# Block 0's sums on GpSimd cut to one and one copy given to ScalarE, next rows requested ahead of the kept transpose, last offset sums held: one change in three parts

## Chip, cores, metric

The kernel runs on one core of a Trainium2 chip. The metric is the device time of one execution in microseconds (us), median over several executions.

## The reference

Two layers of a small graph network over 128 graphs of 64 nodes with 768 features, all in float32:

```python
h = relu(layernorm(x))
for l in range(2):                                   # 2 layers
    m_left, m_right = h @ W_left[l].T, h @ W_right[l].T
    u = lower/upper mix of (h @ m_left.T) and (h @ m_right.T), / sqrt(768)
    attention = exp(u) * adj, each row divided by its sum
    ctx = attention @ (h @ W_lin[l].T + b_lin[l])
    h = relu(ln_a[l] * (ctx - mean) / (std + 1e-3) + ln_b[l])
return x + h
```

(The lines are shortened; shapes are x 128 x 64 x 768, adj 128 x 64 x 64, each weight 2 x 768 x 768.)

## The kernel before

The rows are cut into 16 blocks of 512. A product of 768 x 768 is split into 3 x 3 x 2 pieces and done with 15 instead of 18 groups of multiplications, so each block needs sums of weight pieces (once a layer) and sums of token pieces (once a block). TensorE does the groups, GpSimd most token sums, VectorE and ScalarE the rest. Three places matter here.

The first block. Rows arrive in four tiles; each gets statistics (VectorE), a shift column `nb` (VectorE), a scaling (ScalarE), six transposes (TensorE) and copies out of PSUM. Then the weight and token sums must be ready before TensorE's groups:

```python
START = (0, 2, 1, 3)
# in transpose_rows(0, 0): statistics, column and scaling of tile after tile, then
def turn(n, q):                 # transposes of tile q, then two copies out
    ...
    for m, p in enumerate(banks):
        ...
        (nc.vector.tensor_copy if n < 2 else nc.scalar.copy)(to, ...)
for n, q in enumerate(START):
    todo.append(lambda n=n, q=q: turn(n, q))
...
# the sums; GpSimd's are held until a column is done, by a small copy that reads it
ws, vs = sums_w(0, "l", nc.gpsimd), sums_w(0, "l", nc.vector)
hold(KEEP["nb"][:, START[-2]:START[-2] + 1])
for f in ws[:2]:                # two weight sums on GpSimd
    f()
t, w = deque(sums_t((1, 0, 0), nc.vector)), deque(vs[2:])   # all others on VectorE
needs = ("twtwt", "ttwww", ...)  # what VectorE does ahead of which group
```

The block change. During block u, the rows of block u+1 are normalised, transposed and stored ("kept") in DRAM; the kept transpose is read back as `ht`, and the rows of block u+2 are requested into the freed row tiles. All of these requests stand in one queue, SyncE's:

```python
todo = transpose_rows(l, u, sp)            # ends with the four stores
todo.append(lambda: load_h(1, l, u))       # ht: reads the kept transpose back, 1536 KB
if u + 1 < NB:
    todo.append(lambda: load_rows(l, u + 1, sp))   # eight tiles of 192 KB
...
todo.append(lambda: load_adj(u))           # two transfers of 128 KB
```

The last block. The residual rows and the offset are added ahead of time on GpSimd, at two slots of the plan:

```python
for xs, slot in zip(XS[u, 1], (26, 45)):
    put(slot, lambda xs=xs: nc.gpsimd.tensor_add(xs, xs, rows["b"]))
```

## Time and profile before

| | before |
|---|---|
| time, median of 3 (later 4) executions | 2754.47 us, 2753.4 to 2755.24 (2754.31) |
| span of the profiled execution (a separate one; it took 2756.64 us, more than any of those) | 2754.9 us |
| TensorE busy | 2730.8 us, 99% |
| TensorE idle, all of it | 24.1 us |

How to read it: in the profile's lines PE is TensorE, PEld its weight loads, DVE VectorE, ACT ScalarE, POOL GpSimd and SPq SyncE's queue of requests; L429 is line 429 of the kernel's file, and X, Y, Z, V and aux name banks of PSUM. The bracket behind a TensorE row gives the idle time before it and what ended it. Two more readings of the kernel before: first the transfers of the rows, from the last part of the page (KB each, median us from issue to landing):

```profile
x<-in_x_dram SPq DMA_DIRECT2D x120, 192.0 KB, 8.3
```

Then the stretch around the first scores, in windows of two microseconds: the window and its length, the busy time of PE, PEld, DVE, ACT and POOL with their instructions, the granted TensorE clock, the DMA engines' busy share (a transfer is counted where it starts, so it can pass 1), GB/s.

```profile
70.00:72.00 2.00, 2.00 (x83) 1.67 (x85) 1.93 (x6) 0.00 (x0) 1.92 (x2) 1.00 1.09 207
72.00:74.00 2.00, 2.00 (x95) 1.78 (x84) 0.19 (x1) 0.00 (x0) 2.00 (x3) 1.00 0.41 69
74.00:76.00 2.00, 0.24 (x12) 0.24 (x16) 0.00 (x0) 0.00 (x0) 2.00 (x2) 1.00 0.00 0
```

The third column is TensorE's: it all but stops from 74 to 76 with its operands ready, while the DMA engines have just fallen silent. The trace of the DMA queue that carries TensorE's instructions has one packet at 73 to 73.5, the next block of them.

### The profile page before, as it was taken

The numbers are of one execution on the slowest core, as the hardware profiler recorded it, in microseconds if no ns is written. First come the engines' busy times: TensorE is split into PE (matmuls) and PEld (weight loads), VectorE is DVE, ScalarE is ACT, GpSimd is POOL, SyncE is SP. The second block draws the span as 40 slices with busy tenths as digits, with TensorE's granted clock in tenths as the row PEclk, the third lists the DMA queues.
The fourth block names the chain that finished last, engine by engine and source line by source line (L and its number), as shares of the span: only waits on it lengthen the run. The fifth ranks groups of instructions, "written<-read, shape, count | busy, mean of one in ns | idle before, by whom it ended". The sixth has DMA issues, their size and how long they took to land.

```text
span 2754.9 us, 46440 instructions
## 1 busy us (share of the span) xinstructions
PE 2730.8 (99%) x18746; PEld 2343.7 (85%) x18746; DVE 1348.2 (49%) x2267; ACT 850.2 (31%) x1611; POOL 1195.0 (43%) x937
## 2 busy tenths in 40 slices
PE   9999999999999999999999999999999999999998
PEld 7888888888888888888788888888888888888886
DVE  6555445545454333333435444444444335676666
ACT  3222223222221154454621211121122214444443
POOL 3332352224223555555522344223222325887885
PEclk9999999999999999999999999999999999999999
DMA  6434433343332333343555433443344204555655
GB/s 203 121 75 97 121 82 81 87 120 93 76 76 77 102 104 121 119 146 123 152 129 150 99 75 76 109 119 78 76 98 120 59 26 146 167 165 164 178 161 144
DMA packets 234072, 310.82 MB, mean 113 GB/s; under 512 B 54146, under 2 KB 184450, under 8 KB 225666
## 3 DMA queue, kind: packets, MB, share of 16 engines
q1 hardware_dynamic: 233698, 307.45, 41.6%
q8 instruction: 149, 2.44, 0.4%
q14 instruction: 65, 0.53, 0.1%
q10 hardware_dynamic: 160, 0.39, 0.0%
HBM read 202.91 MB, written 104.86 MB: 112 GB/s over the span
## 4 chain that ended last, share of the span: by engine, by line
PE 96%; DVE 2%; ACT 1%; issue 1%; DMA 0%; SPq 0%; DVEq 0%; ACTq 0%
PE X L429 24%; PE V L429 16%; PE X L839 12%; PE Y L429 12%; PE Z L429 8%; PE V L839 8%; PE Y L839 6%; PE aux L456 5%; PE Z L839 4%; PE aux L654 2%; PE aux L677 1%; PE Y L677 0%; ACT xb L311 0%; DVE wm L470 0%; DMA x<-in_x_dram 0%
## 5 line engine op out<-in xcount | busy, mean ns | idle before, releaser
L155 POOL TENSOR_TENSOR ts<-ht 128x512 f32<-128x512 f32 x441 | 587.6, 1342 | 1223.0 <-DMA ht<-h 503.2
L203 ACT ACTIVATE m<-X 128x512 f32<-128x512 f32 (+1 forms) x256 | 151.7, 593 | 1089.9 <-PE X L429 571.2
L155 POOL TENSOR_TENSOR ts<-ht,ts 128x512 f32<-128x512 f32 x189 | 249.1, 1326 | 135.5 <-PE X L839 60.5
L155 DVE TENSOR_TENSOR m<-m,V 128x512 f32<-128x512 f32 (+1 forms) x256 | 173.4, 677 | 268.0 <-PE V L429 267.9
L155 DVE TENSOR_TENSOR m<-m,X 128x512 f32<-128x512 f32 (+1 forms) x256 | 162.9, 678 | 248.9 <-PE X L429 248.3
L839 PE MATMUL X<-w_n,ts 128*128 128x256 f32 x1024 | 244.2, 380 | 0.8 <-ACT hl L203 0.6
L429 PE MATMUL X<-ts,w_l 128*128 128x256 f32 x1024 | 242.7, 380 | 0.8 <-DVE ts L155 0.7
L429 PE MATMUL X<-ts,w_r 128*128 128x252 f32 (+1 forms) x1024 | 238.8, 376 | 0.1
L155 DVE TENSOR_TENSOR m<-m,Z 128x512 f32<-128x512 f32 (+1 forms) x128 | 87.5, 684 | 307.0 <-ACT m L203 248.7
L839 PEld LDWEIGHTS X<-w_n,ts 128*128 128x128 f32 x1024 | 191.5, 190 | 32.9 <-issue 3.1
L429 PEld LDWEIGHTS X<-ts,w_l 128*128 128x128 f32 x1024 | 192.0, 190 | 31.0 <-DVE m L155 2.7
L429 PEld LDWEIGHTS X<-ts,w_r 128*128 128x128 f32 x1024 | 192.0, 190 | 26.4 <-DVE m L155 0.5
L275 ACT ACTIVATE ht<-ht,b_col,a_col 128x512 f32<-128x512 f32 x192 | 143.5, 804 | 147.0 <-DMA ht<-h 147.0
L839 PE MATMUL Y<-w_n,ts 128*128 128x256 f32 x768 | 182.5, 379 | 0.0
L429 PE MATMUL Y<-ts,w_l 128*128 128x256 f32 x768 | 181.5, 379 | 0.2 <-DVE w_l L155 0.2
L429 PE MATMUL Y<-ts,w_r 128*128 128x252 f32 (+1 forms) x768 | 179.1, 376 | 0.0
L839 PEld LDWEIGHTS Y<-w_n,ts 128*128 128x128 f32 x768 | 145.8, 190 | 20.4 <-issue 0.6
L429 PEld LDWEIGHTS Y<-ts,w_l 128*128 128x128 f32 x768 | 145.8, 190 | 20.3 <-DVE w_l L155 0.6
L429 PEld LDWEIGHTS Y<-ts,w_r 128*128 128x128 f32 x768 | 145.9, 190 | 17.4
L155 DVE TENSOR_TENSOR hl<-hl,V 128x512 f32<-128x512 f32 (+1 forms) x136 | 89.1, 655 | 129.4 <-PE V L839 112.1
L805 POOL TENSOR_TENSOR z<-z,b 128x768 f32<-128x768 f32 x62 | 112.1, 1818 | 80.5 <-DVE z L802 80.5
L203 ACT ACTIVATE hl<-X 128x512 f32<-128x512 f32 (+1 forms) x135 | 78.0, 577 | 222.0 <-PE X L839 218.9
(165 smaller groups left out, 4741.1 us busy)
## 6 DMA issues: line engine op xcount, KB each, us to landing
ht<-h SPq DMA_DIRECT2D x63, 1536.0 KB, 7.1
h<-xb SPq DMA_DIRECT2D x124, 384.0 KB, 6.0
z<-z SPq DMA_DIRECT2D x128, 192.0 KB, 3.1
x<-z SPq DMA_DIRECT2D x128, 192.0 KB, 8.5
x<-in_x_dram SPq DMA_DIRECT2D x120, 192.0 KB, 8.3
xr<-in_x_dram SPq DMA_DIRECT2D x120, 192.0 KB, 3.7
out_dram<-xr SPq DMA_DIRECT2D x120, 192.0 KB, 2.7
adj<-in_adj_dram SPq DMA_DIRECT2D x64, 128.0 KB, 2.8
```

The lines of the kernel that those rows point to most:

```text
L155: (eng.tensor_add if sign == "+" else eng.tensor_sub)(o, a, b)
L203: nc.scalar.activation(to(o), p, AF.Copy, scale=1.0 if sign == "+" else -1.0)
L275: nc.scalar.activation(ht, ht, AF.Relu, bias=cols[1][:, c:c + 1], scale=cols[0][:, c:c + 1])
L429: nc.tensor.matmul(p[:, g], w[ORDER[i][0]][:, c, g * P:(g + 1) * P], b()[t][:, c, :].rearrange(bs, s=S)[:, :, :ns], start=(new and g == c ...
L456: nc.tensor.matmul(p[h * S + e:h * S + e + 32, q, e:e + 95], ht[:, c, b * S + e:b * S + e + 32], mb[:, e:e + 95], start=(c == 0), stop=(c ...
L654: nc.tensor.matmul(cx[k][i, m, :HH], at[j, q, :], hl[j, q, m * HH:(m + 1) * HH], start=True, stop=True)
L677: nc.tensor.matmul(parts[r, k][n][i], at[j, q, :], hl[j, q, cut], start=True, stop=True)
L805: nc.gpsimd.tensor_add(zs[k], zs[k], rows["b"])
L839: nc.tensor.matmul(p[:, n], b[t][:, c, r * P:(r + 1) * P], w[s][:, c, :], start=(i in FIRST and i not in PRELOAD and n == c == 0), stop=(c ...
```

## The change

Intent: (1) in block 0, let GpSimd do one weight sum instead of two, gated so that it no longer holds VectorE's last column, and give one of VectorE's copies to ScalarE; (2) in layer one, request the next rows ahead of the read-back of the kept transpose, so that the DMA engines are free when the scores start; (3) hold the last block's two offset sums until the output tile before them is done, so that they no longer block VectorE.

```diff
--- before.py
+++ after.py
@@ -334,6 +334,9 @@
                     todo.append(inv[q])
                     if after is not None:
                         todo.append(dev[after])
+                    if q == START[2]:
+
+                        todo.append(lambda: turn(0, START[0]))
                     todo.append(norms[q])
         if (l, u) == (0, 0):
             ht = HT[key] = big.tile([P, C, T], F32, name="ht")
@@ -352,10 +355,10 @@
                 for m, p in enumerate(banks):
                     to = ht[:, 3 * m:3 * m + 3].rearrange("p c (a g s) -> p g c a s", a=4, g=2)
                     to = to[:, q // 2, :, q % 2 * 2:q % 2 * 2 + 2, :]
-                    (nc.vector.tensor_copy if n < 2 else nc.scalar.copy)(
+                    (nc.vector.tensor_copy if n == 1 or n < m else nc.scalar.copy)(
                         to, p[:, :3 * P].rearrange("p (c a s) -> p c a s", c=3, a=2))
 
-            for n, q in enumerate(START):
+            for n, q in list(enumerate(START))[1:]:
                 todo.append(lambda n=n, q=q: turn(n, q))
             todo.append(lambda: nc.sync.dma_start(KEPT[l][u], ht))
             return todo
@@ -402,9 +405,9 @@
             def prepare(u):
 
                 todo = transpose_rows(l, u, sp)
-                todo.append(lambda: load_h(1, l, u))
-                if u + 1 < NB:
-                    todo.append(lambda: load_rows(l, u + 1, sp))
+                then = [lambda: load_h(1, l, u)] + ([lambda: load_rows(l, u + 1, sp)] if u + 1 < NB else [])
+
+                todo.extend(then if l else then[::-1])
                 todo.extend(softmax(u - 2) if u > 1 else [])
                 todo.append(lambda: load_adj(u))
                 todo.extend(none * ((9 if u > 1 else 15) if l else 0))
@@ -522,12 +525,11 @@
 
 
                 ws, vs = sums_w(0, "l", nc.gpsimd), sums_w(0, "l", nc.vector)
-                hold(KEEP["nb"][:, START[-2]:START[-2] + 1])
-                for f in ws[:2]:
-                    f()
-                t, w = deque(sums_t((1, 0, 0), nc.vector)), deque(vs[2:])
-
-                needs = ("twtwt", "ttwww", "wwww", "w", "tw", "t", "ww", "ww", "tt", "", "tt")
+                hold(KEEP["nb"][:, START[-1]:START[-1] + 1])
+                ws[0]()
+                t, w = deque(sums_t((1, 0, 0), nc.vector)), deque(vs[1:])
+
+                needs = ("twwtwt", "ttwww", "wwww", "w", "tw", "t", "ww", "ww", "tt", "", "tt")
                 for i, what in enumerate(needs, -1):
                     for f in [(t if c == "t" else w).popleft() for c in what]:
                         if i < 0:
@@ -698,8 +700,15 @@
                 put(1, lambda: load(1))
                 put(6, lambda: nc.gpsimd.tensor_scalar_mul(rows["-b"], rows["b"], -1.0))
                 put(20, lambda: load(0))
-                for xs, slot in zip(XS[u, 1], (26, 45)):
-                    put(slot, lambda xs=xs: nc.gpsimd.tensor_add(xs, xs, rows["b"]))
+
+                def offset():
+
+                    t = stat.tile([P, 1], F32, name="hold", bufs=1)
+                    nc.gpsimd.tensor_copy(t, XS[u - 1, 1][1][:, :1])
+                    for xs in XS[u, 1]:
+                        nc.gpsimd.tensor_add(xs, xs, rows["b"])
+
+                put(42, offset)
 
             def finish_last(u, r):
```

## The prediction

> **What bounds the kernel now.** I read the page's busy shares first, then the chain that ended last, then the TensorE rows of the timeline that have idle time before them, then all engines around those rows.
>
> ```profile
> PE 2730.8 (99%) x18746; PEld 2343.7 (85%) x18746; DVE 1348.2 (49%) x2267; ACT 850.2 (31%) x1611; POOL 1195.0 (43%) x937
> ...
> PE 96%; DVE 2%; ACT 1%; issue 1%; DMA 0%; SPq 0%; DVEq 0%; ACTq 0%
> ```
>
> The page: TensorE is busy 2730.8 of 2754.9 us and is 96% of the chain. The change leaves TensorE's matmuls alone, so it can only win from the 24.1 us in which TensorE is idle, less whatever new idle time it makes. Even all of it is 0.9%: no 2% verdict is in reach. The question is where the idle time lies, and the timeline of TensorE says:
>
> ```profile
> 14.32 1.97 PE L429 MATMUL X<-ts,w_l 128*128 128x256 f32 x8 [0.74 <-DVE ts L155]
> 19.89 1.99 PE L429 MATMUL Y<-ts,w_l 128*128 128x256 f32 x8 [0.16 <-DVE w_l L155]
> 23.37 1.97 PE L429 MATMUL X<-ht,w_l 128*128 128x256 f32 x8 [1.48 <-DVE w_l L155]
> ...
> 75.76 0.85 PE L456 MATMUL aux<-m,ht 128*32 128x95 f32 x29 [1.76 <-issue]
> ...
> 2726.07 1.10 PE L839 MATMUL V<-w_n,ts 128*128 128x256 f32 x4 [1.88 <-DVE hl L155]
> ```
>
> Columns: start, time, what, and in brackets the idle time before it and what ended it. The three parts of the change aim at three of these places: the first block (waits for VectorE's sums, 1.48 us at 23.37), the first block change (1.76 us at 75.76), the last block (1.88 us at 2726.07). Everything between runs from matmul to matmul with gaps under 0.5 us.
>
> **What the Trainium skill says.** (1) "SBUF — State Buffer", section Who interferes with whom: a VectorE instruction with two SBUF inputs contends with a GpSimd instruction that reads SBUF; whichever starts first holds the shared ports for its whole instruction and the other fully blocks; with at most one SBUF input (outside the two-port modes) VectorE does not contend. This trace agrees: the final max-and-add (L816, two SBUF inputs) takes 0.94 us alone and 2.02 and 2.16 us when a GpSimd sum runs; the copies out of PSUM at 11.51 take 0.49 us beside a GpSimd sum, as without one. (2) "DMA: Bandwidth & Descriptors", section Queues, rings and completion order: on each DMA engine, descriptors are consumed in ring order, so what is asked first is served first. The trace fits: rows asked for at 59.25, just behind a 1536 KB transfer, took 7.7 us and more to land. (3) "Runtime: NRT & Kernel Launch", section Instruction fetch mechanics: instructions are fetched by DMA in blocks of 16 KiB, 256 instructions. The instruction queue here moved 2.44 MB in 149 packets, 16.4 KB each, so it agrees.
>
> **Part 1, the first block: about -0.1 us.** Timeline of the kernel before:
>
> ```profile
> 10.30 2.50 POOL L155 TENSOR_TENSOR w_l<-w_l,w_l 128x512 f32<-128x512 f32 x2
> 10.34 1.24 DVE L294 SCALAR_TENSOR_TENSOR nb<-mv,rs 128x1 f32<-128x1 f32 x1
> ...
> 11.51 1.94 DVE L355 COPY ht<-aux 128x384 f32<-128x384 f32 x4
> ```
>
> A one-column instruction (0.16 us elsewhere) is held 1.1 us by GpSimd's sum; then four copies of 0.485 us pitch; then VectorE runs sums without a pause, one each 0.60 us: token sum at 13.48, a weight sum at 14.09, the second token sum at 14.69, and so on to the weight sum that ends TensorE's wait at 23.37. So this part is worth what the second token sum moves.
> After: GpSimd's gate is the last row tile's column, so it cannot hold that column's instruction. One copy moves to ScalarE, one is pulled ahead of the column. But in the built program the pulled VectorE copy waits for ScalarE's copy of the same tile. Working: ScalarE's copy 10.04 to 10.51 (0.47 as at 12.55), VectorE's copy 10.55 to 11.04, reciprocal and column to 11.35, two copies to 12.3. GpSimd's gate at 11.49, its one sum from 11.64 to 12.89. The first token sum, ready at 12.3, now meets that sum and is held to about 12.78 (L816's held cases resumed some 0.13 us before GpSimd's end). Then the weight sum that came over from GpSimd (0.60), the other weight sum (0.60), and the second token sum at 12.78 + 3 x 0.60 = 14.58, against 14.69. The hold moves from one instruction to another and the extra sum eats the copies that went: 0.1 us. TensorE's first group starts at some 13.6 instead of 14.32, but gives that back in the later waits.
>
> **Part 2, next rows ahead of the kept transpose: about +0.5 us.** Timeline at the first block change:
>
> ```profile
> 58.80 0.35 SPq L268 DMA_DIRECT2D ht<-h  x1
> ...
> 66.05 2.49 POOL L155 TENSOR_TENSOR ts<-ht 128x512 f32<-128x512 f32 x2 [9.87 <-DMA ht<-h]
> ...
> 68.35 1.70 PEld L429 LDWEIGHTS X<-ts,w_l 128*128 128x128 f32 x8
> ```
>
> The stores (issued 46.95 to 52.2) must land before ht is read back at 58.80; it lands at 66.05, GpSimd's first sum takes 1.27 us, to 67.3, and TensorE wants it at 68.35. Slack: 1.0 us. (At a later change GpSimd starts at 395.84 and TensorE wants the sum at 405.6: slack 8.5 us.)
> *Gain.* In the two-microsecond windows the DMA engines are at 100% from 62 to 72 with the eight row tiles behind ht, and the block of TensorE instructions for the scores is fetched only at 73 to 73.5, 2.6 to 3.1 us after the scores began at 70.38 (0.2 to 2.9 us at four other changes, so this sign is weak; that the engines were full only here is the stronger one). With the rows asked for at 52.2 the engines should be quiet by 70, and the 1.76 us shrink to 0.3 or less: -1.5 us.
> *Cost.* Rows now stand between stores and ht. Windows: the stores fill the engines (0.78 to 0.96) from 48 to 57; rows alone move at 221 GB/s (68 to 70), so 1.57 MB take 7.1 us, 57 to 64.1; ht moves at 424 GB/s (62 to 64), 3.7 us, 64.1 to 67.8. Before, the same sum put ht's data at 60 to 64.3 and the landing at 66.05. So the landing goes 3.3 us later, to some 69.3, less whatever 57 to 60, now idle, hides better than I assume; the first sum ends at 70.6, the slack of 1.0 us is gone, and TensorE waits 2.2 us at its first group of the second block. I take 2.0: 2.0 - 1.5 = +0.5 us. All later changes of layer one have the slack to hide 3.3 us.
>
> **Part 3, the held offset sums: -1.1 us.** Timeline of the end:
>
> ```profile
> 2721.76 1.82 POOL L702 TENSOR_TENSOR ht<-ht,b 128x768 f32<-128x768 f32 x1 [0.61 <-DMA ht<-in_x_dram]
> ...
> 2722.38 2.02 DVE L816 SCALAR_TENSOR_TENSOR xr<-z,xr 128x768 f32<-128x768 f32 x1
> ...
> 2725.52 0.41 DVE L155 TENSOR_TENSOR hl<-hl,V 128x256 f32<-128x256 f32 x1
> ...
> 2732.25 1.83 POOL L702 TENSOR_TENSOR ht<-ht,b 128x768 f32<-128x768 f32 x1
> 2732.72 2.16 DVE L816 SCALAR_TENSOR_TENSOR xr<-z,xr 128x768 f32<-128x768 f32 x1
> ```
>
> L816 is held by the offset sum until it ends. Without it: 0.94 instead of 2.02, -1.08 us, and VectorE's next rows follow in line up to the sum at 2725.52 that frees bank V, for which TensorE waited 1.88 us. That wait falls to 0.8. From there to the end TensorE's groups follow each other, so the end moves by 1.08. The second hold (2732.72) cost TensorE nothing visible; its removal gives at most 0.2.
> The two sums now run back to back, behind a gate (some 0.2 us) once the last output tile before them is done, some 2734.5 to 2738.2 in the new time. VectorE then reads PSUM and one SBUF operand and is not held. GpSimd's next two sums end at about 2741.7 instead of 2741.3 (2742.38 - 1.08), before VectorE uses the second at some 2742.4. Not on the path.
>
> Sum: -0.1 + 0.5 - 1.1 = -0.7 us: 2754.47 becomes 2753.8 us.
>
> **Rivals.** (a) *Part 2 wins outright*: if the rows overlap the stores better, ht lands before 67 and only the fetch gap's 1.5 us stays: 2752 us, or a little under. For it: 57 to 60 was almost idle before (shares 0.35, 0.27). Against it: row tiles never moved above 258 GB/s while alone or with stores. (b) *Part 2 loses*: ht lands near 70, and the fetch gap was not the DMA's doing (other changes show 0.3 to 0.5 us of it with quiet engines): +2.5 to 3, total 2756. (c) *Part 1 wins 0.5 us*: if VectorE's first token sum slips in ahead of GpSimd's sum; then GpSimd is the one held, for 0.7 us at most: 2753.3. (d) *Vector work is not the end of the last wait*: something else frees bank V and part 3 gives nothing: 2754.9; the trace names VectorE's sum, so I give it little.
>
> **Range and chances.** Parts 1 and 3 have some 0.4 us of doubt each, part 2 some 1.7 us; the runs before spread over 1.8 us. Together 2751.6 to 2755.6. A 2% change would be 55 us; the idle time has 24: within 2% is near certain.
>
> **What would show it.** Part 3 right: both L816 rows near 0.94 us, TensorE's wait at V near 0.8. Part 2 right: ht landing near 69 and a TensorE wait for GpSimd's sum of some 2 us just ahead of the first scores, with the 1.76 us gap gone. Part 1 right: no held column instruction, a held first token sum, and still some 1.5 to 2 us of wait at the fifth group. It would be wrong if ht kept its 66 us landing, or if a later change of block also waited for ht.

## The result, and the profile after

The changed kernel took 2755.42 us, median of 4 executions (2754.34 to 2756.81); the kernel before took 2754.31 (2753.4 to 2755.24, 4 executions). The ratio is 1.0004, with a 95% interval of 0.9987 to 1.0022: the same. The predicted 2753.8 us was 1.6 too low, and the result lies inside the range, close to its upper end.

The parts did not come out alike. The page after, busy times:

```profile
PE 2730.5 (99%) x18746; PEld 2343.2 (85%) x18746; DVE 1347.9 (49%) x2267; ACT 849.9 (31%) x1612; POOL 1192.3 (43%) x937
```

TensorE's instructions are as many as before, 18746. The idle stretches moved. TensorE's rows in the timeline after, where those of before had 0.16, 1.48, 1.76 and 1.88:

```profile
19.38 1.99 PE L432 MATMUL Y<-ts,w_l 128*128 128x256 f32 x8 [0.74 <-DVE w_l L155]
22.85 1.96 PE L432 MATMUL X<-ht,w_l 128*128 128x256 f32 x8 [1.48 <-DVE w_l L155]
...
71.02 2.46 PE L432 MATMUL X<-ts,w_l 128*128 128x256 f32 x8 [2.82 <-POOL ts L155]
73.41 5.27 PE L459 MATMUL aux<-m,ht 128*32 128x95 f32 x192
...
2725.13 1.10 PE L848 MATMUL V<-w_n,ts 128*128 128x256 f32 x4 [0.82 <-DVE hl L155]
```

The wait at bank V fell by 1.06 us. The fetch gap of 1.76 us in the scores is gone, but ahead of them stands a new wait of 2.82 us for GpSimd's sum. Also the rows after it are longer: the group took 2.46 us (1.89 in the kernel before) and the scores 5.27. The windows after show why:

```profile
70.00:72.00 2.00, 0.98 (x5) 0.88 (x6) 1.18 (x4) 0.00 (x0) 2.00 (x2) 1.00 0.01 4
72.00:74.00 2.00, 2.00 (x21) 1.30 (x23) 0.00 (x0) 0.00 (x0) 1.92 (x3) 0.60 0.00 0
74.00:76.00 2.00, 2.00 (x64) 2.00 (x60) 0.00 (x0) 0.00 (x0) 1.92 (x2) 0.55 0.03 8
```

The granted clock was at half from 72.41 to 75.82 by the trace's clock records. Why the sum came late is in the transfers: the read-back and what waited for it in the timeline, and the landing times of the rows on the page.

```profile
59.23 0.43 SPq L268 DMA_DIRECT2D ht<-h  x1
...
69.70 2.48 POOL L155 TENSOR_TENSOR ts<-ht 128x512 f32<-128x512 f32 x2 [14.08 <-DMA ht<-h]
```

```profile
x<-in_x_dram SPq DMA_DIRECT2D x120, 192.0 KB, 5.4
```

The rows land earlier (5.4 us after their request instead of 8.3) and the kept transpose 3.65 us later at this change of block (GpSimd starts at 69.70 instead of 66.05). At no later change does TensorE wait for such a sum.

The start of the kernel after, on VectorE and GpSimd:

```profile
10.60 0.16 DVE L294 SCALAR_TENSOR_TENSOR nb<-mv,rs 128x1 f32<-128x1 f32 x1
...
11.05 1.28 POOL L155 TENSOR_TENSOR w_l<-w_l,w_l 128x512 f32<-128x512 f32 x1
...
11.73 1.15 DVE L155 TENSOR_TENSOR ts<-ht 128x512 f32<-128x512 f32 x1
```

The last column takes 0.16 us instead of 1.24; now the first token sum is held, 1.15 us instead of 0.69. And the end:

```profile
2722.50 0.95 DVE L825 SCALAR_TENSOR_TENSOR xr<-z,xr 128x768 f32<-128x768 f32 x1
...
2734.65 3.58 POOL L709 TENSOR_TENSOR ht<-ht,b 128x768 f32<-128x768 f32 x2
```

The max-and-add takes 0.95 us instead of 2.02, and the offset sums run at 2734.65, where they hold nobody.

Single executions differ by 1 to 2 us. Part of this is TensorE's instruction fetch, which shows gaps of 0.2 to 0.8 us at other scores, in layer two as well, where only the last block was changed. The two profiled executions also differ in rank: the one before (2756.64 us) was slower than all four others of its kernel, the one after (2755.69) near its median. That is how the profile after can have a shorter span (2753.9 us) than the one before (2754.9), although the median is longer.

### The profile page after: what moved, and what is told of

Read it like the earlier page. It is cut to its first block, busy times and chain, and to the rows that moved or that the text cites. A ratio compares the mean times of both kernels' runs of the same rounds, so it can differ in the third digit from the quotient of the medians.

```text
span 2753.9 us, 46427 instructions
## 1 busy us (share of the span) xinstructions
PE 2730.5 (99%) x18746; PEld 2343.2 (85%) x18746; DVE 1347.9 (49%) x2267; ACT 849.9 (31%) x1612; POOL 1192.3 (43%) x937
## 4 chain that ended last, share of the span: by engine, by line
PE 95%; DVE 1%; POOL 1%; issue 1%; ACT 0%; DMA 0%; SPq 0%; DVEq 0%; POOLq 0%; ACTq 0%
PE X L432 23%; PE V L432 16%; PE X L848 12%; PE Y L432 12%; PE Z L432 8%; PE V L848 8%; PE Y L848 6%; PE aux L459 5%; PE Z L848 4%; PE aux L656 2%; PE aux L679 1%; POOL w_r L155 1%; PE Y L679 0%; POOL ts L155 0%; DVE wm L473 0%
## 5 line engine op out<-in xcount | busy, mean ns | idle before, releaser
L155 DVE TENSOR_TENSOR hl<-hl,X 128x512 f32<-128x512 f32 (+1 forms) x136 | 83.2, 653 | 129.2 <-PE X L848 125.1
```

What stands on the lines that cost most here:

```text
L155: (eng.tensor_add if sign == "+" else eng.tensor_sub)(o, a, b)
```

## The experiments

Twelve kernels ran. The first two calls ran on one chip, the third on another, where the kernel before itself was slower and more scattered. All results were correct. Times are medians with lowest and highest:

| run | kernel | time, us | executions | ratio to before [95%] |
|---|---|---|---|---|
| | before, calls 1 and 2 | 2754.03 and 2754.04 (2753.37 to 2755.75) | 9, then 10 (the same 9 and one more) | |
| e1_start | part 1 alone | 2754.04 (2752.35 to 2754.5) | 5 | 0.9999 [0.9985, 1.0013] |
| e2_rows | part 2 alone | 2755.13 (2754.57 to 2757.79) | 5 | 1.0007 [0.9995, 1.002] |
| e3_held | part 3 alone | 2752.62 (2752.15 to 2753.65) | 5 | 0.9996 [0.9983, 1.0008] |
| e4_no_rows | parts 1 and 3 | 2752.62 (2752.14 to 2753.68) | 5 | 0.9995 [0.9983, 1.0008] |
| e9_change_again | the change | 2755.66 (2753.57 to 2758.34) | 6 | 1.0005 [0.9992, 1.0017] |
| e5_rows_after_first | part 3, and part 2 from the second block change on; no part 1 | 2753.06 (2752.01 to 2755.1) | 4 | 0.9997 [0.9984, 1.0011] |
| e6_early | part 3, half the rows much earlier | 2751.94 (2751.6 to 2752.09) | 4 | 0.9992 [0.9979, 1.0006] |
| e7_filler | the change and 10 idle transposes | 2754.05 (2753.22 to 2756.3) | 4 | 1.0001 [0.9988, 1.0015] |
| | before, call 3 | 2755.7 (2753.8 to 2757.33) | 9 | |
| e10_before_again | before | 2755.91 (2754.24 to 2758.78) | 5 | 1.0 [0.9986, 1.0014] |
| e11_later | the change, read-back later still | 2757.39 (2756.17 to 2758.86) | 5 | 1.0007 [0.9995, 1.002] |
| e12_later_filled | the same and 48 idle transposes | 2757.87 (2756.41 to 2759.91) | 5 | 1.0009 [0.9997, 1.0022] |
| e13_no_gpsimd | parts 1 and 3, no GpSimd sum in block 0 | 2753.91 (2753.49 to 2756.44) | 5 | 0.9996 [0.9984, 1.0009] |

Every interval holds 1, so no total here is a proven difference by itself. What is claimed below rests on the traces, and on times only where the lists of single executions hardly overlap.

### Each part alone, and the change without part 2

The edits are the parts of the diff above: e1_start has the hunks on `turn`, `START` and the sums; e2_rows the hunk in `prepare`; e3_held the hunk in the last block; e4_no_rows the first and the last of these.

> Part 1 alone. My theory (the hold only moves from the one-column instruction to the first token sum, so nothing is won): from the end of the third row tile's column instruction on VectorE to TensorE's fifth weight group is 13.4 +- 0.1 us, as before (13.36), and the total is within 0.3 us of before. Rival (part 1 wins what its shorter list of copies saves, 0.5 us): 12.9 us and 0.5 us faster. The first wait gap of the last block (1.88 us) and the 1.76 us at the first block change stay.

> Part 2 alone. My theory: it is the loss of the change. TensorE waits 2.5 to 3 us for GpSimd's first sum at the first block change, and where that idle time lets the granted clock fall to one half, another 1.5 to 1.7 us are lost, against the 1.76 us gap that goes: total 1 to 2.5 us slower than before. Rival (part 2 is neutral, the later block changes give back what the first costs): the total is within 0.3 us of before, and the fetch gaps of blocks 2 to 15 of layer one shrink by 1 us or more together in this run as they did in the change's own profile.

> Part 3 alone. My theory: both held max-and-add rows go to 0.95 us, TensorE's wait in the last block goes from 1.88 to 0.82 us, total 1.06 us faster. Rival (the end is set by something else): same wait gone, but the distance from TensorE's group at 2714.8 to the last instruction stays at 36.0 us, total as before.

> Parts 1 and 3 without part 2. If part 2 is what eats the gain: 0.7 to 1.3 us faster than before and 1.5 to 2.5 us faster than the change. Rival (part 2 neutral, the rest is noise of the fetch gaps): as fast as the change within 0.5 us.

**Part 3** is the one that gains: 2752.62 alone and with part 1, against 2754.03, 1.4 us. All executions but one of each of these two kernels lie below the lowest of the nine of before (2753.37). The wait at V was 0.82 us in e3_held and 0.81 in e4_no_rows; in e1_start and e2_rows, without part 3, it was 1.66 and 1.81. The rival fell: from the last block's first group into V from `ht` (2714.61 in the profile before) to the last instruction it was 40.25 us before and 39.17 in e3_held.

**Part 1** gains nothing. A clean measure is the time from the start of the third column's instruction on VectorE to the start of TensorE's fifth group, since it leaves out when the first rows landed. Without part 1: 13.52 us in the kernel before, 13.52 in e2_rows, 13.51 in e3_held. With it: 13.61 in the profile after, 13.58 in e4_no_rows and 14.04 in e1_start. In e1_start the first row tile was scaled late, TensorE's transposes of it with it, and then ScalarE's new copy made VectorE wait:

```profile
10.27 0.56 DVE L358 COPY ht<-aux 128x384 f32<-128x384 f32 x1 [0.96 <-ACT ht L358]
```

VectorE idled for 0.96 us (0.54 in the profile after) and the last column came at 10.93, 1.79 us after the third column (9.14); in the profile after that distance is 1.36. So the expectation missed: it counts from the end of that column's instruction, 13.4 within 0.1 us, and here that is 13.88, away from the rival's 12.9 too. The times agree that the part is worth nothing: 2754.04 with it against 2754.03, and 2752.62 with and without it beside part 3.

**Part 2** costs: 2755.13 alone, 1.1 us over before, and all five executions lie above eight of the nine of before. The expected wait of 2.5 to 3 us with a half clock did not show in its profile, whose TensorE rows have a shorter wait and the clock at 1.00; but the profiled execution was the fastest of the five (2754.57), and the two slow ones, 2757.43 and 2757.79, were not profiled:

```profile
69.64 1.99 PE L429 MATMUL X<-ts,w_l 128*128 128x256 f32 x8 [1.21 <-POOL ts L155]
71.56 4.55 PE L456 MATMUL aux<-m,ht 128*32 128x95 f32 x192
```

The rival's smaller fetch gaps cannot be told: TensorE's idle stretches of over 0.15 us from 80 to 2700 us sum to 1.7 us here and to 3.1 in the profile before, but to 1.9 in e3_held, which has no part 2.

### The control, and the rows ahead only from the second block change on

e9_change_again is the change, unaltered. e5_rows_after_first has this line in place of the change's; it also has part 3, but not part 1, though its expectation speaks of the change:

```diff
-                todo.extend(then if l else then[::-1])
+                todo.extend(then if l or u == 1 else then[::-1])
```

> The whole change once more, unaltered, as the control for the three other runs on this chip. All theories: same state as before, about 2755 us, 0.5 to 1.5 us above the kernels without the moved rows (2752.6 earlier). The kept transpose lands at 68 to 70, TensorE waits 1.2 to 2.8 us for GpSimd's sum ahead of block 1's first token group. Theory (idle brings the half clock): if that wait is near 2.8 us, the granted clock in 72 to 76 falls to 0.5 to 0.6 again; if it is near 1.2, the clock stays at 1.00. Rival (the clock drop was one execution's accident): no relation between the two.

> The change, but at the first block change the next rows stay behind the kept transpose; at all later changes of layer one they go ahead of it. Theory A (part 2 costs at the first block change only, since every later one has slack): as fast as without part 2, 2752.6 within 0.5, landing of the kept transpose at 64 to 66, no TensorE wait for the sum. Theory B (rows ahead also cost something at the later changes): near the whole change, 2755. Theory C (rows ahead gain at later changes): under 2752.

The control took 2755.66 us, and its executions scatter over 4.8 us. On the same chip, though earlier, the change without part 2 (e4_no_rows) took 2752.62: by that part 2 cost 3.0 us. The expected 0.5 to 1.5 was too small. The profiled execution was the slowest of the six and shows the worst case:

```profile
71.79 3.78 PE L432 MATMUL X<-ts,w_l 128*128 128x256 f32 x8 [3.22 <-POOL ts L155]
75.50 5.12 PE L459 MATMUL aux<-m,ht 128*32 128x95 f32 x192
```

The wait was 3.22 us, and the clock was at half from 70.78 to 77.61, so the half clock set in during the wait.

e5_rows_after_first took 2753.06, with one execution at 2755.1; the median is 0.4 above part 3 alone (e3_held, from which it differs by the later rows only) and 2.6 below the control, which has part 1 besides. No TensorE wait for the sum is left in its trace. So part 2's cost arises at the first block change, as the first theory had it; a loss or a gain of some tenths at the later ones cannot be told from the scatter.

### Is the half clock a consequence of the wait?

e7_filler adds this to the change (the result is never read):

```diff
+                    if l == 0 and u == 1 and k == 0 and i == 0:
+                        fill = ps_st.tile([P, 2 * TH], F32, name="Y")
+                        for _ in range(10):
+                            nc.tensor.transpose(fill[:, :P], KEEP["ident"], KEEP["ident"])
```

> The whole change plus ten transposes of the identity on TensorE just ahead of block 1's first token group (their result is never read), so that TensorE is not idle so long while it waits for GpSimd's sum. Theory A (the long idle stretch brings the half clock on top of the wait): the wait is still there, partly filled, the granted clock in 72 to 76 stays at 1.00, the group after it takes 1.9 and not 2.5 us, and the time is 0.5 to 1.7 us under the whole change: 2753.3 to 2754.5. Rival B (the clock has nothing to do with idle time): clock and time as the whole change, 2755 or up to 0.5 us more. Rival C (most executions wait only 1.2 us and never fall to half clock): clock at 1.00 in both, times equal within 0.4.

It took 2754.05 us against the control's 2755.66, and its profile shows the clock at 1.00 throughout, a remaining idle stretch of 0.36 us, the group at 1.99 and the scores at 4.51. But the ranges overlap, and in this execution the read-back had landed early (68.27), so that the bare wait would have been some 1.5 us. This did not settle it. So the next pair makes the read-back late on purpose, once bare and once with fillers:

```diff
                 then = [lambda: load_h(1, l, u)] + ...
+                if (l, u) == (0, 1):
+                    then.insert(1, lambda: load_adj(u))    # asked for ahead of the read-back
...
-                todo.append(lambda: load_adj(u))
+                if (l, u) != (0, 1):
+                    todo.append(lambda: load_adj(u))
```

e12_later_filled is e11_later with the filler loop at 48.

> The whole change, made worse on purpose: at the first block change the adjacency too is asked for ahead of the kept transpose, so that TensorE surely waits long for GpSimd's sum. 2 MB of adjacency at 220 to 420 GB/s is not all, the request counts 1 MB: 2.5 to 4.8 us later landing, 72 to 74, wait 5 to 8 us. Theory A (a long idle stretch brings the half clock): granted clock 0.50 to 0.60 for the group and scores after the wait, group 3.5 us or more instead of 1.9. Rival B (clock drop was chance): clock 1.00 after the wait.

> The same as the one made worse, plus 48 transposes of the identity on TensorE in the wait (some 5 to 6 us at the 0.11 to 0.125 us of one; their result is never read). Theory A: the sum comes as late as without them, but the clock stays at 1.00, the group after it takes 1.9 us, and the whole is 1.5 to 3 us faster than without the fillers, though it does more work. Rival B: the same time as without them, or slower.

The adjacency is only two transfers of 128 KB, as the page lists it, not the 1 MB taken in the expectation, so the read-back landed at 69.06 and not at 72 to 74. The wait of 2.12 us still brought the half clock. TensorE's row and the windows of e11_later:

```profile
70.38 3.68 PE L435 MATMUL X<-ts,w_l 128*128 128x256 f32 x8 [2.12 <-POOL ts L155]
```

```profile
70.00:72.00 2.00, 1.62 (x4) 1.35 (x5) 1.25 (x4) 0.00 (x0) 1.92 (x3) 0.61 0.02 4
72.00:74.00 2.00, 2.00 (x7) 1.14 (x6) 0.00 (x0) 0.00 (x0) 2.00 (x2) 0.53 0.00 0
```

And e12_later_filled, where the sum came even later (read-back at 70.13) but TensorE had work:

```profile
68.44 5.40 PE L435 MATMUL Y<-ident 128*128 128x128 f32 x48
...
73.68 1.89 PE L439 MATMUL X<-ts,w_l 128*128 128x256 f32 x8
...
75.51 4.13 PE L466 MATMUL aux<-m,ht 128*32 128x95 f32 x192
```

```profile
70.00:72.00 2.00, 2.00 (x21) 2.00 (x20) 1.56 (x5) 0.00 (x0) 1.87 (x2) 1.00 0.04 12
72.00:74.00 2.00, 2.00 (x19) 1.98 (x18) 0.00 (x0) 0.00 (x0) 1.92 (x3) 1.00 0.00 0
```

The group took 1.89 us instead of 3.68. So idle time ahead of the group is what brings the half clock, and the rival falls. The time missed its expectation: 2757.87 against 2757.39, no gain, because 48 fillers were too many. GpSimd's first sum was ready at 71.4 (70.13 plus 1.25, half of its two), TensorE finished the fillers at 73.68, and the 2.3 us between ate what the clock gave back.

Over the traces: idle 1.21 us, clock kept (e2_rows); 2.12, 2.82 and 3.22 us, clock halved (e11_later, after, e9_change_again) for 3.4, 3.4 and 6.8 us. From the start of the group to the end of the scores it took 5.96 us at full clock (e12_later_filled, 73.68 to 79.64), and 7.93, 7.66 and 8.83 us in the three halved ones: 1.7 to 2.9 us lost on top of the wait.

A fourth case lies in the kernel before itself. In e10_before_again, described below, TensorE waited 1.90 us at bank V in the last block, and a stretch at half clock followed:

```profile
2726.53 1.10 PE L839 MATMUL V<-w_n,ts 128*128 128x256 f32 x4 [1.90 <-DVE hl L155]
```

```profile
2727.94:2731.35 3.41, 3.41 (x10) 2.69 (x9) 2.28 (x4) 1.05 (x3) 2.19 (x2) 0.50 0.97 271
```

The first profile of the same kernel waited 1.88 us there and kept its clock. The difference is where the wait falls. In all fourteen traces the clock records change only at multiples of 3.41 us from the first record. Cut into such windows, TensorE was idle for 2.12 us (e11_later, 67.04 to 70.46), 2.03 (after, 69.00 to 72.41), 2.21 (e9_change_again, 67.37 to 70.78) and 1.90 (e10_before_again, 2724.53 to 2727.94) in the windows just before the four drops. In all windows after the first record that full clock followed, up to the last matmuls, it was idle for 1.81 us at most (e2_rows, 2721.70 to 2725.11); of the 1.88 us wait 1.67 lay in one window. By these figures the idle time within one window decides, and nearly the same wait can halve the clock in one execution and not in the next. (In e9_change_again a window at half clock with 1.01 us of idle time was followed by another at half.) It also means that part 3 can win more than its 1.06 us: the half clock of e10_before_again cost some 1.7 us more at the end.

### What the rows were moved for: the fetch gap

e6_early asks for half of block 2's rows (four of eight tiles) already in block 0, at 30 us, into a tile of their own; the other half stays behind the read-back. It has part 3, but not part 1 or 2.

```diff
+        for g in range(2) if part is None else (part,):
+            if (l, u, g) == (0, 2, 0):
+                t = pool.tile([P, 2, H], F32, name="x2", bufs=1)
...
-                    todo.append(lambda: load_rows(l, u + 1, sp))
+                    todo.append(lambda: load_rows(l, u + 1, sp, 1 if (l, u) == (0, 1) else None))
...
                 cols.extend([column("a_col", ln_a[0]), column("b_col", ln_b[0])])
+                load_rows(0, 2, sp, 0)
```

> Part 3 alone, plus half of block 2's rows requested in block 0, while the DMA engines are quiet, in a tile of their own; the other half stays behind the kept transpose. Theory A (what was wanted of part 2 was to keep the DMA engines free when the scores' instructions are fetched, but that fetch normally costs only 0.3 us): no gain over part 3 alone, 2752.6 within 0.4; fetch gap at the first scores 0.3 us as without it. Theory B (full DMA engines delay the fetch by 1.5 us in most executions): 1 to 1.5 us faster than part 3 alone, about 2751.3. Kept transpose lands at 64 to 66 under both.

It took 2751.94, and all its four executions (2751.6 to 2752.09) lie under all five of e3_held (2752.15 to 2753.65, earlier on the same chip). This is 0.7 us better than part 3 alone, between the two expectations. The read-back landed at 64.03, no wait followed, and the scores ran in one piece:

```profile
69.72 4.28 PE L461 MATMUL aux<-m,ht 128*32 128x95 f32 x192
```

By then the 1.76 us gap of the kernel before looked like one execution's accident, since e1_start, e3_held, e4_no_rows and e5_rows_after_first, with the same order of requests at this place, had 0.34, 0.36, 0.30 and 0.59. A second profile of the kernel before, unaltered, tests it:

> The kernel before once more, for a second profile of it. Theory A (the 1.76 us of fetch gap in the first scores was that one execution's accident; the same row order with other parts of the change showed 0.30 to 0.59): gap 0.6 or less, kept transpose landing at 64 to 66.5, time 2754.0. Theory B (the gap belongs to the kernel before): gap 1.5 or more.

That expectation failed; the gap was there again:

```profile
76.08 0.85 PE L456 MATMUL aux<-m,ht 128*32 128x95 f32 x29 [1.50 <-issue]
```

The cause lies in front of it. SyncE's wait for the stores to land, ahead of the read-back's request, in e10_before_again and then in e4_no_rows (us in all, number of waits, the longest):

```profile
SPq L268 <- DMA h<-xb: 6.5, 2, 3.3
```

```profile
SPq L268 <- DMA h<-xb: 5.3, 2, 3.3
```

Both profiles of the kernel before have 6.5; e1_start, e3_held, e4_no_rows and e13_no_gpsimd have 5.3, and in e5_rows_after_first and e6_early too the read-back was requested 10.6 to 10.7 us after the first store, against 11.8 in the two of before. With the last store landing 1.2 us later, read-back and rows follow 1.2 us later, and the rows still fill the DMA engines while the scores wait for their next instructions. Set against the start of the scores, the instruction block is in the DMA trace at:

| kernel | scores start | DMA engines under half busy from | instruction block in the trace | gap in the scores |
|---|---|---|---|---|
| before | 70.38 | 72.5 | 73 to 73.5 | 1.76 |
| e10_before_again | 70.97 | 73.5 | 73 to 73.5 | 1.50 |
| e4_no_rows | 70.55 | 72 | 71 to 72 | 0.30 |
| e13_no_gpsimd | 70.62 | 72 | 71 to 72 | 0.35 |
| e5_rows_after_first | 69.88 | 71 | 71 to 72 | 0.59 |
| e6_early | 69.72 | 67 | 70.5 to 71 | none |

So full DMA engines do delay the fetch, and part 2's aim was sound. How much there is to win depends on when the last store lands. Why both profiled executions of the kernel before had the late one, and none of the six others with the same order of requests, is open: e3_held, for one, was edited in the last block only. Both were slow executions of their kernel (2756.64 us against 2753.4 to 2755.24 of the others; 2758.78, the slowest of five), so the late store may come with slow executions only; no run tests it. The times suggest that many executions of the kernel before do not have it (if all had, e3_held should have gained 1.06 plus 1.2 to 1.4 us, and it gained 1.4 in all).

### Is the one GpSimd sum worth keeping?

```diff
-                ws, vs = sums_w(0, "l", nc.gpsimd), sums_w(0, "l", nc.vector)
-                hold(KEEP["nb"][:, START[-1]:START[-1] + 1])
-                ws[0]()
-                t, w = deque(sums_t((1, 0, 0), nc.vector)), deque(vs[1:])
-                needs = ("twwtwt", ...
+                t, w = deque(sums_t((1, 0, 0), nc.vector)), deque(sums_w(0, "l", nc.vector))
+                needs = ("twwwtwt", ...
```

(set against parts 1 and 3)

> Parts 1 and 3, but with no sum on GpSimd in block 0: all weight sums on VectorE. Theory A (with one sum left, GpSimd's help is worth nothing: it takes 0.6 us of adds off VectorE and holds VectorE's token sum by about 0.55): from the third column's start to the fifth group 13.6 us within 0.1, as with one sum; time as parts 1 and 3 with the sum, 2752.6 within 0.4. Rival B (the one sum still helps): 0.5 us longer. Rival C (it hurts): 0.3 us or more shorter.

From the third column to the fifth group it took 13.66 us, as with the one sum (13.58 to 13.66 in five executions, 14.04 and 14.12 in two where the first tile was late). The rows of VectorE and TensorE in e13_no_gpsimd:

```profile
12.39 0.69 DVE L155 TENSOR_TENSOR ts<-ht 128x512 f32<-128x512 f32 x1
...
23.59 1.97 PE L432 MATMUL X<-ht,w_l 128*128 128x256 f32 x8 [1.48 <-DVE w_l L155]
```

The token sum is no longer held (0.69 instead of 1.15 us), and the sum that came over to VectorE takes the time instead. The time, 2753.91, is not inside the expected 2752.2 to 2753.0, since the chip was another one; it is 1.8 us under the kernel before of the same call, where e4_no_rows was 1.4 under.

The fastest version found is e6_early, 2.1 us (0.08%) under the kernel before by the medians.

## Why the prediction was right or wrong

- **What bounds**: right. TensorE was busy 2730.5 us after as well, and everything moved by a few us.
- **Part 3, -1.1 us**: right. Both max-and-adds take 0.95 us, the wait at V is 0.82, which is 1.06 less, and the offset sums hold nobody. e3_held alone measured 1.4; the half clock seen behind this wait in e10_before_again is one way to more than 1.06, not shown to be the reason.
- **Part 1, -0.1 us**: the mechanism was right (no held column, a held token sum, 1.48 us of wait left at the fifth group), the size nearly: +0.06 to +0.14 us in most traces. The step had VectorE's wait for ScalarE's copy, but not that it can grow: where the first row tile is scaled late, VectorE idles for about 1 us instead of 0.54, and the part costs 0.5 to 0.6 us (e1_start, e9_change_again). Rival (c), a gain of 0.5, did not show. e13_no_gpsimd shows that the sum left on GpSimd pays for nothing.
- **Part 2, cost +2.0 us**: the mechanism was right and the term too small. The prediction put the landing at "some 69.3" and the wait at 2.0. (By its own figures, 67.8 against 64.3, ht comes 3.5 and not 3.3 us later, at 69.55; and it rounded a wait of 2.2 down.) Landings were 68.3 to 70.5 and waits 1.21, 2.82 and 3.22. The term left out is the clock: waits of 2.82 and 3.22 us also halved it, for 1.7 us more in the profile after and up to 2.9 in the control.
- **Part 2, gain -1.5 us**: right as to what delays the fetch (the gap was gone after), wrong in taking 1.76 us as the typical loss. Five kernels with the old order here had 0.30 to 0.59.
- **Sum, -0.7 us**: +1.1 was measured there, and +1.6 in the control's call. The step that failed is "2.0 - 1.5 = +0.5" for part 2: alone it measured +1.1 against before, and +3.0 as the control against e4_no_rows. The sign of the sum was wrong, and it stayed inside the range only because the range allowed part 2 1.7 us of doubt. Rival (b), in which part 2 loses 2.5 to 3 us and the total is 2756, came nearest in number, with the landing near 70; its reason, that the fetch gap was not the DMA engines' doing, did not hold.
- **"All later changes of layer one have the slack"**: right by the traces, which have no such wait later, and by e5_rows_after_first within its scatter.

## What to carry to other kernels

When one queue carries both the transfer that somebody waits for next and one that nobody needs yet, moving the second ahead takes slack from the first: look for the change with the least slack (1.0 us here, 8.5 later), and move the transfer to where the engines are idle instead, as e6_early did. A wait of TensorE costs more than its length once the clock halves, so price a new wait of about 2 us or more (1.90 was enough here) with the slower work behind it. And before taking a gap seen in one profile for typical, see how that execution ranks among the others: here both profiles with the large gap were slow ones, so even the second did not make it typical.

## What the Trainium skill lacked or had wrong

- "TensorE: Matmul & The Clock Gate", section What's actually happening, gives a free-running window of 3413 ns and lets the clock halve after at least one idle window (~3.4 us). The halved stretches here, three of 3.4 and one of 6.8 us, agree with one or two such windows. But no wholly idle window was needed: 1.90 to 2.21 us of idle time within one window were enough, and 1.81 us was not. What share of a window suffices is not said there. One halving cost 1.7 to 2.9 us here, beside a wait of 1.9 to 3.2.
- "Runtime: NRT & Kernel Launch", section Instruction fetch mechanics, calls the cost of a block boundary mostly hidden. Here a fetch behind full DMA engines left TensorE without instructions for 1.50 and 1.76 us, and for 0.30 to 0.59 us when they drained sooner; with quiet engines (e6_early) no gap showed. That a fetch waits for data transfers is not said in that section.
- No page was found that explains the last store's landing 1.2 us later in two of eight traces with the same requests (SyncE waited 6.5 against 5.3 us).
